# Where the first local query of the next image is convolved, normed and stacked: within the dense stage instead of the last slots of the image ahead

## The chip, the cores and the metric

One core of a Trainium2 chip runs the whole kernel. The metric is the device time of that core in microseconds, as the median of several runs. One further execution was recorded by the hardware profiler; times of single instructions come from that one. Engines are called PE (TensorE, matmuls), PEld (its weight loads), DVE (VectorE), ACT (ScalarE), POOL (GpSimd) and SP (SyncE, which here only issues DMAs).

## What is computed

The input is four images of 384 channels and 48 x 48 pixels. Every image goes through one attention block whose queries get a local part from a depthwise 7 x 7 convolution (all in fp32):

```python
local = conv_general_dilated(x, conv_w, feature_group_count=C)   # depthwise 7x7, then a batch norm as scale and shift
x_norm = layernorm(x_flat, ln_gamma, ln_beta)                    # over the 384 channels of a pixel
q, k, v = split(x_norm @ qkv_w.T + qkv_b)                        # 8 heads of 48
q = q + layernorm(local_flat, ln_gamma, ln_beta)
attn = softmax(q @ k.T * 48 ** -0.5)
out = x_flat + (attn @ v) @ proj_w.T + proj_b
```

## The kernel before

**Tiles and stages.** The 48 rows of an image are cut into 6 groups of 8 rows, 384 pixels each. A query tile t is one group of one image, so there are 24, and tile t belongs to image t // 6. An array over channels is `[128, 3, 384]`: 128 partitions, 3 chunks of channels, 384 pixels. The work of an image has two kinds of stage.

- The *dense stage* (loop `for gk in range(NG)` at the start of an image's first tile, line 1042) makes keys, values and queries of the image group by group from the normed x, and the output projections of the image before. `from_x` yields twelve times for a group; each call of `both(making)` lets it run over one pair of projections, so a group has six pairs. For the first image this work is written out ahead of the loop over tiles.
- Then each of its six tiles runs 12 *slots*. A slot takes one pair of heads and 6 blocks of 128 keys: `score_batch` (matmuls at L884, then the exponentials on ACT at L892) and `weigh_batch` (matmuls at L899 with the exponentials and the values). Three slots make a pair of heads.

PE, DVE and ACT run their instructions in the order in which the program writes them. The DMAs on SP and POOL are put in an order by the framework's scheduler, which knows their inputs; within each queue they are then issued in that order, and a DMA whose input isn't ready holds the ones behind it.

**The convolution.** `conv_ops(t)` is a generator of 147 DVE instructions for tile t (49 taps of 3 chunks, L288 and L284). All tiles' generators are chained into one `stream`, which runs ahead of the tile that is being attended. `convolve(point)` takes the next so many of them. How many, `plan` works out before: each point in the program (two a slot, five a group of the dense stage) has a `room`, an estimate in us of the DVE time left there (`spare`, `spare_at_keys`), and each tile has a point at which its convolution is `due`. At each point the plan takes the highest rate that any coming due point asks for. A new tile's first instruction also issues the load of the slab of x for the tile after it (`load_slab`, SP, two buffers); the results go to `acc`, of which there are three buffers.

**The norm of the convolved tile** (class `Norm`) is done without matmuls, in steps that are written at different places:

- `sum` adds the three chunks on DVE (L404, L405); `out` transposes and reduces (L460, L461), sends 12 numbers a partition to DRAM (`parts`, L464) and reads them back in the form that sums over partitions (`four`, L465). This exchange is the way of one norm's sums across the partitions; each norm has two.
- `few_centre` waits for `four` (L474) and subtracts the mean (L481, L482); `squares` runs on ACT; `sum_squares` and `out` make the second exchange.
- `few_variance` waits for it (L474, L488); `few_root` is three small ACT instructions (L493 to L495); `few_newton` refines on DVE (L499 to L501).
- `local_end` scales the tile (L734). `query_end` adds it, times the gain, to the query projected from x (L743, three instructions).

The tiles of x for the next image are normed in the same way, under the names `norm_x` (in slots) and `norms_x` (in the dense stage).

**Stacking.** fp32 scores are made of rounded high and low parts. `high_queries(t, p)` rounds on ACT (L756), `low_queries(t, p)` subtracts on DVE (L761) and then issues six SP DMAs (four for the last pair of heads) that put the parts into the rows in which the matmuls want them (L766, L768). `gather_tails` (L517) collects the fourth pair of heads with eight SP DMAs. Every score matmul of a slot reads the stacked query `qs` of its pair of heads. `qs` has five buffers, which residual loads (`load_residual`) and fetched outputs (`fetch`) share.

**Order today.** For tile t + 1 the norm is in the slots of tile t: `sum` at the end of slot 4, `few_centre` at the end of slot 5, `sum_squares` at the end of slot 6, `few_variance` in slot 8, `local_end` in slot 9. Its convolution is due before slot 5. `query_end`, `high_queries` and `low_queries` follow in slot 9 only if t + 1 belongs to the same image. For the first tile of the next image the projected query does not exist yet, so `query_end` stands in group 1 of the dense stage, `high_queries` at its end, and `low_queries` and `gather_tails` at the end of group 2:

```python
            if following and s == second + 1:
                local_end(t + 1, norm.few_newton() if t else norm.newton())
                if g < NG - 1:
                    query_end(t + 1)
                    high_queries(t + 1, 0)
```

In the dense stage `lows_out` makes the low parts of a group's keys (L599) and issues their DMAs: for key chunk 0 eight on SP (`ks<-k`, L533 to L536), for the others on POOL. `finish` adds an output's residual (L865) and stores it from SP (L868).

Of the kernel before, what the change touches and what calls it, by code (L numbers as in the profile page):

```python
# [45 lines left out]
def unshifted_pass(  # L46
# [265 lines left out]
    def norm_slots(t):  # L312
        return (5, 8) if t else (8, 10)

    def spare(t, s, half):
        b, g = divmod(t, NG)
        first, second = norm_slots(t)
        time = 3.6 - (0.0 if half else 0.6) - (0.6 if half and s % 3 == 1 else 0.0)
        if b + 1 < B and g >= later(b + 1):
            time -= {(3, 1): 2.3, (4, 1): 2.2, (5, 1): 2.3, (7, 0): 0.4, (8, 0): 2.6}.get(  # L320
                (s, half), 0.0
            )
        if g:
            time -= {(2, 0): 0.7, (4, 1): 1.4}.get((s, half), 0.0)
        if t == 0:
            time -= {(7, 1): 1.1, (8, 1): 1.4, (9, 1): 1.1, (11, 0): 5.0}.get((s, half), 0.0)
        elif t + 1 < NT:
            time -= {(4, 1): 2.3, (5, 1): 2.2, (6, 1): 2.3, (8, 0): 0.4, (9, 0): 4.5}.get(
                (s, half), 0.0
            )  # L330
        return max(0.3, time)
# [5 lines left out]
    def spare_at_keys(b, g, h):  # L337
        time = 4.6 - {0: 0.6, 2: 0.7, 3: 1.4, 4: 1.2}.get(h, 0.0)
        if g < later(b):
            time -= {0: 2.3, 2: 2.2, 4: 2.3}.get(h, 0.0)  # L340
        if 0 < g <= later(b):
            time -= {1: 0.4, 3: 2.6}.get(h, 0.0)
        return time - {(1, 1): 2.7, (2, 1): 1.4}.get((g, h), 0.0)

    points, room = [], []
    for t in range(NT):
# [3 lines left out]
        points += [("slot", t, s, h) for s in range(NSLOT) for h in range(2)]  # L350
        room += [spare(t, s, h) for s in range(NSLOT) for h in range(2)]
    each = CC * KS * KS
    due = [
        (points.index(("slot", t - 1, norm_slots(t - 1)[0], 0)), t * each) for t in range(1, NT)
    ]
    share = {}

    def plan(done):
# [10 lines left out]
    def convolve(*point):  # L369
        for _ in range(share[point]):  # L370
            next(stream)
# [265 lines left out]
    def both(making):  # L637
        next(making)
        next(making)
# [92 lines left out]
    def local_end(t, rs):  # L732
        acc = accs[t]
        nc.vector.scalar_tensor_tensor(acc, acc, -1.0, rs, ALU.mult, ALU.mult)  # L734
# [300 lines left out]
    for t in range(NT):  # L1035
        b, g = divmod(t, NG)
        if g == 0 and b:

            sums_add()
            load_x(b, NG - 1)  # L1040
            norms_x = {}
            for gk in range(NG):
                before = t - NG + gk
                load_residual(before)
                making = from_x(b, gk, before, ao if gk < NG - 1 else outputs[before][0])
                new = NG - later(b) + gk if gk < later(b) else None
                old = norms_x.get(gk - 1)
                both(making)
                convolve("kv", t, gk, 0)
                if new is not None:  # L1050
                    norms_x[gk] = Norm(xn[b, new])
                    norms_x[gk].sum()
                    norms_x[gk].out()
                both(making)
                if old:
                    old.few_variance()
                    old.few_root()
                if gk == 1:
                    query_end(t)
                    rb = divide(t - 1)  # L1060
                if gk == 2:
                    last_ao = outputs[t - 1][0]
                    nc.vector.tensor_mul(last_ao, last_ao, rb)
                convolve("kv", t, gk, 1)
                both(making)
                convolve("kv", t, gk, 2)
                lows_out(1)
                if new is not None:
                    norms_x[gk].few_centre()
                    norms_x[gk].squares()  # L1070
                both(making)
                convolve("kv", t, gk, 3)
                lows_out(2)
                if old:
                    old.scale(old.few_newton())
                both(making)
                convolve("kv", t, gk, 4)
                if new is not None:
                    norms_x[gk].sum_squares()
                    norms_x[gk].out()  # L1080
                both(making)
                if gk == 1:
                    high_queries(t, 0)
                if gk == 2:
                    low_queries(t, 0)
                    gather_tails(*reversed(queries[t]))
                if gk < NG - 2:
                    ao = fetch(before + 1)
        following = t + 1 < NT
        next_image = b + 1 < B  # L1090
        coming = next_image and g >= later(b + 1)
        first, second = norm_slots(t)
        for s in range(NSLOT):
            pair, third = divmod(s, KB // BATCH)
            if third == 1 and pair < NP - 1:
                high_queries(t, pair + 1)
            score_batch(t, s)
            if pair < NP - 1 or g < NG - 1:
                load_keys(b, (pair + 1) % NP, third)
            if s == 1 and g == 0:  # L1100
                keep_stack(b)
            if s == 2 and g:
                rb = divide(t - 1)
            if s == 0 and coming:
                load_x(b + 1, g - later(b + 1))
            if s == NSLOT - 4 and g == NG - 1:
                if next_image:
                    ao = fetch(t - g)
                    for gx in range(NG - later(b + 1), NG - 1):
                        load_x(b + 1, gx)  # L1110
                else:
                    places = [("acc", 3)] * 3 + [("sq", 2)] * 2 + [("qs", 5)]
                    aos = []
                    for i in range(NG):
                        load_residual(t - g + i, *places[i])
                        aos.append(fetch(t - g + i) if i < g else outputs[t][0])
            if coming and s == X_SLOTS[1] + 1:
                norm_x.scale(norm_x.few_newton())
            if following and s == second + 1:
                local_end(t + 1, norm.few_newton() if t else norm.newton())  # L1120
                if g < NG - 1:
                    query_end(t + 1)
                    high_queries(t + 1, 0)
            if coming and s == X_SLOTS[0] + 1:
                jobs.extend(norm_x.square_jobs())
            if following and s == first + 1:
                jobs.extend(norm.square_jobs())
            if coming and s == X_SLOTS[1]:
                norm_x.few_variance()
            if t and following and s == second:  # L1130
                norm.few_variance()
            convolve("slot", t, s, 0)
            sums_add()
            if t == 0 and s in (first, second):
                norm.mean_kept()
            if coming and s == X_SLOTS[1]:
                norm_x.few_root()
            if following and s == second:
                norm.few_root() if t else norm.root()
            if s == first and t == 0:  # L1140
                norm.centre()
            weigh_batch(t, s)
            if third == 1 and pair < NP - 1:
                low_queries(t, pair + 1)
            convolve("slot", t, s, 1)
            if following and s == second + 1 and g < NG - 1:
                low_queries(t + 1, 0)
                gather_tails(*reversed(queries[t + 1]))
            if coming and s == X_SLOTS[0]:
                norm_x.few_centre()  # L1150
            if t and following and s == first:
                norm.few_centre()
            if s == OUT_SLOT and g:
                ao = outputs[t - 1][0]
                nc.vector.tensor_mul(ao, ao, rb)  # L1155
                hold(t - 1)
            if coming and s == X_SLOTS[0] - 1:
                norm_x = Norm(xn[b + 1, g - later(b + 1)])
                norm_x.sum()
                norm_x.out()  # L1160
            if coming and s == X_SLOTS[0] + 1:
                norm_x.sum_squares()
                norm_x.out()
            if following and s == first - 1:
                norm = Norm(accs[t + 1])
                norm.sum()
                if t:
                    norm.out()
            if following and s == first + 1:
                norm.sum_squares()  # L1170
                if t:
                    norm.out()
# [559 lines left out]
```

## Time and profile before

| | us |
|---|---|
| median of 3 runs | 2858.98 |
| lowest and highest | 2855.88, 2863.1 |
| the profiled execution, its own time | 2855.57 |
| its span in the profile | 2853.8 |
| PE busy | 2769.0 (97%) |
| DVE busy | 2459.7 (86%) |
| ACT busy | 1636.8 (57%) |
| granted PE clock, mean over the span | 0.985 |

A busy figure is the time in which an engine has an instruction running; matmuls overlap, so a busy PE need not be at its peak. Tile t's slots begin, by the first score matmul of each tile, at 164.8 us for tile 0, 280.8 for tile 1, 690.9 for tile 5, 931.9 for tile 6, 1607.9 for tile 12 and 2283.2 for tile 18. The dense stages of images 1, 2 and 3 end at the last three of these times.

### The profile page before, as it was taken

The numbers are of one execution on the slowest core, as the hardware profiler recorded it, in microseconds if no ns is written. First come the engines' busy times: TensorE is split into PE (matmuls) and PEld (weight loads), VectorE is DVE, ScalarE is ACT, GpSimd is POOL, SyncE is SP. The second block draws the span as 40 slices with busy tenths as digits, with TensorE's granted clock in tenths as the row PEclk, the third lists the DMA queues.
The fourth block names the chain that finished last, engine by engine and source line by source line (L and its number), as shares of the span: only waits on it lengthen the run. The fifth ranks groups of instructions, "written<-read, shape, count | busy, mean of one in ns | idle before, by whom it ended". The sixth has DMA issues, their size and how long they took to land.

```text
span 2853.8 us, 53591 instructions
## 1 busy us (share of the span) xinstructions
PE 2769.0 (97%) x19238; PEld 1740.4 (61%) x19238; DVE 2459.7 (86%) x4875; ACT 1636.8 (57%) x2638; POOL 592.9 (21%) x1125
## 2 busy tenths in 40 slices
PE   9987989999899999999999999999999999999999
PEld 6654656565555666665655666666665566666665
DVE  7789998989899999997998999998888998998502
ACT  4344656565522666676642467666672276676662
POOL 5720000000057200010026401000005710010000
PEclk9998999999999999999999999999999999999999
DMA  7444444553445554445536545455454555444541
GB/s 140 106 135 117 125 128 134 151 151 101 140 117 162 166 175 140 149 144 162 153 100 182 166 144 155 168 157 145 133 150 133 153 159 167 149 144 167 163 161 63
DMA packets 197461, 410.57 MB, mean 144 GB/s; under 512 B 69888, under 2 KB 140480, under 8 KB 196672
## 3 DMA queue, kind: packets, MB, share of 16 engines
q0 software_dynamic: 65440, 254.88, 26.7%
q1 hardware_dynamic: 128752, 148.55, 21.2%
q8 instruction: 154, 2.52, 0.4%
q10 hardware_dynamic: 2992, 3.62, 0.4%
q14 instruction: 123, 1.01, 0.1%
HBM read 298.44 MB, written 64.78 MB: 127 GB/s over the span
## 4 chain that ended last, share of the span: by engine, by line
PE 78%; DVE 14%; DMA 5%; issue 1%; ACT 0%; SPq 0%; POOL 0%; ACTq 0%; DVEq 0%; POOLq 0%
PE o L899 32%; PE r L884 26%; PE r L511 20%; DVE acc L288 10%; DMA parts<-part 2%; DMA four<-parts 2%; DMA qs<-qs 1%; DVE sq L405 0%; DVE sq L460 0%; DVE ao L803 0%; DVE part L461 0%; DMA start_up<-in_qkv_wT_dram 0%; DVE sq L404 0%; DVE acc L482 0%; DVE ao L1155 0%
## 5 line engine op out<-in xcount | busy, mean ns | idle before, releaser
L288 DVE SCALAR_TENSOR_TENSOR acc<-slab,vec,acc 128x368 f32<-128x368 f32 (+6 forms) x3447 | 1767.1, 581 | 1.2
L892 ACT ACTIVATE pt<-r 128x768 f32<-128x768 f32 x1728 | 1250.0, 829 | 150.2 <-PE r L884 120.7
L899 PE MATMUL o<-pt,v 128*64 128x384 f32 x6912 | 1184.4, 492 | 0.0
L884 PE MATMUL r<-qs,ks 64*128 64x384 f32 x10368 | 1016.7, 345 | 67.0 <-DMA qs<-qs 38.9
L884 PEld LDWEIGHTS r<-qs,ks 64*128 64x128 f32 x10368 | 905.9, 188 | 256.9 <-issue 210.6
L899 PEld LDWEIGHTS o<-pt,v 128*64 128x64 f32 x6912 | 473.0, 137 | 592.9 <-issue 516.0
L568 POOL DMA_DIRECT2D ks<-wide x276 | 199.3, 724 | 1819.4 <-PE r L884 1768.6
L784 ACT COPY o<-o 113x384 f32<-113x384 f32 x192 | 91.9, 479 | 379.0 <-PE o L899 379.0
L511 PE MATMUL r<-xn,w_qk 128*128 128x384 f32 x864 | 283.7, 486 | 0.0
L511 PEld LDWEIGHTS r<-xn,w_qk 128*128 128x128 f32 x864 | 164.3, 190 | 114.3
L511 PE MATMUL r<-w_v,xn 128*128 128x384 f32 x432 | 145.1, 488 | 0.7 <-ACT w_v L697 0.5
L588 ACT COPY v<-r 128x384 f32<-128x384 f32 x72 | 32.1, 480 | 193.0 <-PE r L511 193.0
L803 DVE TENSOR_TENSOR ao<-ao,o 113x384 f32<-113x384 f32 x144 | 79.4, 551 | 54.8 <-ACT o L784 54.7
L511 PE MATMUL r<-af,w_o 128*128 128x384 f32 x360 | 119.1, 487 | 0.0
L511 PEld LDWEIGHTS r<-w_v,xn 128*128 128x128 f32 x432 | 81.6, 190 | 59.2 <-issue 2.4
L474 DVE TENSOR_REDUCE few<-four 128x12 f32<-128x48 f32 x80 | 18.5, 231 | 107.9 <-DMA four<-parts 107.5
L794 ACT COPY ao<-o 113x384 f32<-113x384 f32 x72 | 34.5, 479 | 125.4 <-PE o L899 125.4
L536 POOL DMA_DIRECT2D wide<-k x192 | 96.7, 508 | 9.2 <-issue 5.5
L511 PEld LDWEIGHTS r<-af,w_o 128*128 128x128 f32 x360 | 68.3, 190 | 47.8 <-issue 0.6
L558 POOL DMA_DIRECT2D wide<-k x192 | 93.1, 491 | 9.5 <-DMA wide<-k 6.8
L552 POOL DMA_DIRECT2D wide<-k x144 | 70.6, 493 | 97.6 <-ACT k L596 69.2
L613 ACT ACTIVATE xn<-r,qkb 128x384 f32<-128x384 f32 x72 | 40.8, 578 | 78.1 <-PE r L511 76.6
(129 smaller groups left out, 1160.7 us busy)
## 6 DMA issues: line engine op xcount, KB each, us to landing
ks<-wide POOLq DMA_DIRECT2D x276, 768.0 KB, 7.1
qs<-qs SPq DMA_DIRECT2D x528, 48.0 KB
xr<-in_x_dram SPq DMA_DIRECT2D x24, 576.0 KB
slab<-in_x_dram SPq DMA_DIRECT2D x32, 378.0 KB
wide<-k POOLq DMA_DIRECT2D x480, 24.0 KB, 2.1
held<-ao SPq DMA_DIRECT2D x20, 576.0 KB
af<-held SPq DMA_DIRECT2D x20, 576.0 KB
rb<-rden SPq DMA_DIRECT2D x48, 216.0 KB
```

Of the source, the lines that this page charges most:

```text
L288: nc.vector.scalar_tensor_tensor(dst, src, weight, dst, ALU.mult, ALU.add)
L511: nc.tensor.matmul(dst, lhsT=weights(c), rhs=src(c), start=c == 0, stop=c == CC - 1)
L536: queue.dma_start(out=dst[r + 32 * i : r + 32 * i + 32, 1], in_=k[r + 16 : r + HD, 1])
L552: nc.gpsimd.dma_start(out=last[16 * u : 16 * u + 16, 0], in_=k[r : r + 16, 0])
L558: nc.gpsimd.dma_start(out=last[to : to + 16, 1], in_=k[r : r + 16, 1])
L568: nc.gpsimd.dma_start(out=stacks[b, p].bitcast(F32)[:, :, at], in_=wide[b, p][:, :, at])
L613: nc.scalar.activation(src[:, i, :], q[:, :G], AF.Identity, bias=qkb[:, 0, i : i + 1])
L784: nc.scalar.copy(part[0 : 64 + HA], sums[0 : 64 + HA, 0, :G])
L803: nc.vector.tensor_add(dst, dst, part[0 : 64 + HA])
L884: nc.tensor.matmul(r[:, j, :G], lhsT=ks[rows, w, kb * P : (kb + 1) * P], rhs=qs[rows, m, :], start=i == 0, stop=i == 2,)
L892: nc.scalar.activation(pt, r[:, :, :G], AF.Exp, scale=SCALE)
L899: nc.tensor.matmul(sums[halves[j], 0, :G], lhsT=values[t // NG, kb // NB][:, first : first + 64], rhs=pt[:, j, :], start=i == 0, stop=i == ...
```

## The change

For the first tile of images 1, 2 and 3 (tiles 6, 12 and 18) the whole norm moves from the slots of the tile ahead (5, 11 and 17) into groups 4 and 5 of the dense stage, and `query_end` and the stacking move there too, from groups 1 and 2 to group 5. The point at which the convolution of these tiles is due moves to the start of group 4, and the estimates of room follow; the shares of all points change with that. In the last tile of an image nothing is done for a following tile any more. Every other tile's order stays.

```diff
@@ in spare, spare_at_keys and the due points
-        elif t + 1 < NT:
+        elif g < NG - 1:
...
-        return time - {(1, 1): 2.7, (2, 1): 1.4}.get((g, h), 0.0)
+        return time - {
+            (1, 1): 1.0, (2, 1): 1.4, (4, 0): 2.3, (4, 2): 2.2, (4, 4): 2.3, (5, 0): 0.4,
+            (5, 1): 4.5, (5, 2): 0.6,
+        }.get((g, h), 0.0)
...
-    due = [
-        (points.index(("slot", t - 1, norm_slots(t - 1)[0], 0)), t * each) for t in range(1, NT)
-    ]
+    due = []
+    for t in range(1, NT):
+        last = ("slot", t - 1, norm_slots(t - 1)[0], 0) if t % NG else ("kv", t, 4, 0)
+        due.append((points.index(last), t * each))
@@ in the dense stage, for gk in range(NG)
                     norms_x[gk].sum()
                     norms_x[gk].out()
+                if gk == 4:
+                    norm = Norm(accs[t])
+                    norm.sum()
+                    norm.out()
                 both(making)
...
                 if gk == 1:
-                    query_end(t)
                     rb = divide(t - 1)
+                if gk == 5:
+                    norm.few_variance()
+                    norm.few_root()
...
                 convolve("kv", t, gk, 1)
+                if gk == 5:
+                    local_end(t, norm.few_newton())
+                    query_end(t)
+                    high_queries(t, 0)
                 both(making)
                 convolve("kv", t, gk, 2)
                 lows_out(1)
...
+                if gk == 4:
+                    norm.few_centre()
+                    norm.squares()
+                if gk == 5:
+                    low_queries(t, 0)
+                    gather_tails(*reversed(queries[t]))
                 both(making)
...
+                if gk == 4:
+                    norm.sum_squares()
+                    norm.out()
                 both(making)
-                if gk == 1:
-                    high_queries(t, 0)
-                if gk == 2:
-                    low_queries(t, 0)
-                    gather_tails(*reversed(queries[t]))
...
-        following = t + 1 < NT
+        following = g < NG - 1
@@ in the slots
                 local_end(t + 1, norm.few_newton() if t else norm.newton())
-                if g < NG - 1:
-                    query_end(t + 1)
-                    high_queries(t + 1, 0)
+                query_end(t + 1)
+                high_queries(t + 1, 0)
...
-            if following and s == second + 1 and g < NG - 1:
+            if following and s == second + 1:
                 low_queries(t + 1, 0)
```

## The prediction

> **What bounds the kernel now.** I read the busy time by stage first, one window for each query tile, because the page's 97% for PE is a mean over stages with different limits. Columns: window, its length, then busy us (instructions) of PE, PEld, DVE, ACT, POOL, then granted PE clock, DMA share, GB/s.
>
> ```profile
> 280.80:382.40 101.60, 95.05 (x720) 61.10 (x720) 94.52 (x186) 61.12 (x93) 8.65 (x12) 0.94 0.42 120
> 382.40:487.70 105.30, 95.49 (x724) 60.36 (x722) 97.70 (x192) 61.38 (x94) 8.64 (x12) 0.94 0.43 130
> ...
> 586.50:690.90 104.40, 94.47 (x724) 59.09 (x722) 91.57 (x192) 62.67 (x100) 8.64 (x12) 0.95 0.46 133
> 690.90:792.40 101.50, 93.88 (x723) 59.38 (x721) 89.29 (x184) 62.63 (x99) 5.13 (x16) 0.95 0.43 127
> 792.40:931.90 139.50, 139.50 (x434) 82.08 (x432) 131.33 (x255) 34.75 (x72) 89.50 (x184) 1.00 0.54 147
> 931.90:1020.50 88.60, 88.60 (x721) 56.65 (x720) 85.73 (x168) 60.36 (x93) 15.98 (x27) 1.00 0.54 167
> ```
>
> Rows one to four are tiles 1, 2, 4 and 5 (image 0), then the first dense stage, then tile 6. An undisturbed tile takes 88.3 us of unbroken matmuls; the dense stage is also unbroken. Image 0's tiles take 99 to 105 us. The list of waits, asked for VectorE in the same windows, says who sets that: in tile 5 DVE waited 11.1 us for `four<-parts`, in tile 4 11.8, in tile 2 7.0, in tile 1 6.5. Busy plus that wait is 100.4 of 101.5 us in tile 5, 103.4 of 104.4 in tile 4, 104.7 of 105.3 in tile 2: **VectorE sets image 0, TensorE everything after it.**
>
> The wait in tile 5 belongs to the very norm that the change moves. Timeline of VectorE, then of TensorE:
>
> ```profile
> 737.59 0.55 DVE L803 TENSOR_TENSOR ao<-ao,o 113x384 f32<-113x384 f32 x1
> 749.23 0.23 DVE L474 TENSOR_REDUCE few<-four 128x12 f32<-128x48 f32 x1 [11.09 <-DMA four<-parts]
> ...
> 747.22 1.84 PE L884 MATMUL r<-qs,ks 64*128 64x384 f32 x18
> 753.27 0.79 PE L884 MATMUL r<-qs,ks 64*128 64x384 f32 x6 [4.21 <-ACT ao L794]
> 754.39 2.29 PE L884 MATMUL r<-qs,ks 64*128 64x384 f32 x12 [0.33 <-ACT pt L892]
> 756.61 6.14 PE L899 MATMUL o<-pt,v 128*64 128x384 f32 x24
> ```
>
> VectorE waits at `few_centre`, ScalarE's squares of that norm wait behind it, and PE stalls; the 24 `weigh` matmuls after it take 6.14 us, not 4.09.
>
> Last, the nearest thing to what the change builds: the start, where the query of tile 0 is stacked right at the end of the first dense work. TensorE, VectorE, then SP's queue:
>
> ```profile
> 164.83 0.65 PE L884 MATMUL r<-qs,ks 64*128 64x384 f32 x1 [8.31 <-issue]
> 166.34 5.20 PE L884 MATMUL r<-qs,ks 64*128 64x384 f32 x35 [0.85 <-DMA qs<-qs]
> ...
> 152.76 1.14 DVE L743 SCALAR_TENSOR_TENSOR xn<-acc,of_ln,xn 128x384 f32<-128x384 f32 x2
> 157.57 0.56 DVE L761 TENSOR_TENSOR qs<-xn,qs 128x384 fp32r<-128x384 f32 x1 [3.67 <-ACT qs L756]
> ...
> 152.87 3.04 SPq L517 DMA_DIRECT2D qt<-xn  x5
> 157.56 0.51 SPq L768 DMA_DIRECT2D qs<-qs  x1
> 162.99 1.49 SPq L768 DMA_DIRECT2D qs<-qs  x2
> ```
>
> `query_end` ends at 153.9, `low_queries` at 158.1, the last stacking DMA is issued by 164.5, and scores run freely from 166.34: **12.4 us after `query_end`, 8.2 after `low_queries`.** Today the other images pay none of this, since their first query is stacked in groups 1 and 2, over 60 us ahead.
>
> **What the Trainium skill says.** "TensorE: Matmul & The Clock Gate", section "What's actually happening": after an idle window of about 3.4 us the clock falls to half and needs a busy window to return. The trace agrees: the granted clock is 0.83 over 748 to 768 us, around that stall, so 3.4 us lost on top of its 4.5 us of idle time. "DMA: Bandwidth & Descriptors", section "Issuing engines are not separate DMA queues": DMAs of SP and POOL share the same 16 engines. The trace agrees: `four<-parts`, 24 KB, landed 11 us after its issue while a slab and key stacks were moving. "Perfetto Trace Analysis", section "Sequencer Loop": an engine takes instructions in order and each waits for its semaphores; so a late one holds all behind it, as in tile 5.
>
> **The change, part by part.** The plan's shares are worked out from the code's own arithmetic; a conv instruction costs 0.52 us by pace (25 in 12.87 us).
>
> *Conv moved out of image 0.* Tiles 1 to 4 get 1, 4, 3 and 12 instructions fewer: 20 x 0.52 = 10.4 us, all on VectorE where it sets the time: **-10.4**.
>
> *Tile 5.* Removed: `sum` and `sum_squares` with `out` (2 x 2.3), `few_centre` (2.1), `few_variance` (0.4), newton and `local_end` (2.3): 9.4 us, and the wait of 11.1. Added: 4 conv, 2.1. VectorE falls from 100.4 to about 82, under TensorE's 88.3. The tile ends at 88.3 to 90: **-12**. The norm of x stays there; a wait of up to 4 us of its own would fit in the room.
>
> *Tiles 11 and 17* lose the same norm for 12 and 15 conv. They stand at 89.8 and 88.8: at most **-2**. Tiles 18 to 21 get 6 to 8 conv more (4 us); VectorE is at 80 to 82 of 88.3 there, tile 6 ran unbroken at 85.7, so 0; without that room up to 4 us each.
>
> *Tiles 10 and 16.* The next conv tile, so its slab load, now begins at slot 5, between the two exchanges of their norm; before it began at slot 1. VectorE waited 8.0 us for one exchange in tile 10, which cost that tile 5.0 us. Tile 4, with the slab there, took 11.2 us from part to four, tile 10 without it 11.4, tile 5 with it 13.8. So 0 to 2.5 us more each, times 1.3 for the clock: **+3** (0 to +7). A gain is excluded, as no instruction left that stretch.
>
> *Dense stages, VectorE's sum.* 19, 19 and 12 conv fewer (10 us) against 9.4 us of norm: 0. `query_end`, the copies and stacking DMAs only change place within the stage. Group 4 now has two exchanges; those of x in this stage took 5.3 to 7.9 us from part to landing, and some 7 us of other VectorE work lies between, so waits of 0 to 2. In the first dense stage tile 8's slab load comes right behind the second exchange, as in tile 5: 8 to 11 us there.
>
> *Dense stages, the end.* Let E be the end of dense matmuls (931.9, 1607.9, 2283.2). ScalarE evacuates the second pair of group 5 by E-14.4. `few_root` queues behind it: 0.75, E-13.65. Newton, `local_end`, `query_end`: 4.2 us in the rows from 997.84 to 1001.93, so E-9.4. ScalarE's `high_queries` follows at E-8.9; it waits for `query_end`, and the evacuation of keys 1 and 2 waits behind it, some 3 us later than now, covered by free PSUM buffers. Then 6 conv (3.1), one `low` (0.6), `low_queries` (0.55): E-5.2. SP has 20 issues of 0.62 us in this stretch: 8 of `gather_tails` and 2 stackings that need only the high part, from E-10.4 to E-4.3; 6 `ks<-k` of the same `low`, to E-0.6; the 4 stackings left, to E+1.9. They land 1.9 us (the start) to 5 us (tile 5's stacking) later: **E+5.4** by the middle. Nothing hides it: all scores of slot 0 need this query. Groups' output additions, later on VectorE by as much, hold the fourth PSUM buffer until about E+4, so an early landing would not make it free.
>
> *Buffers and POOL.* The query's `qs` buffer is free for four groups longer, and `acc` of tile 6 is held four groups longer: three are in use when tile 8 begins in group 5, tile 9 begins in slot 11, after tile 7's is freed. POOL's stores of keys 1 and 2 start some 3 us later; those keys are wanted from slot 3 on. PE waited for none of these in the dense stage, so 0 either way.
>
> The second stage adds 0 to 2.4 for its second exchange (middle 1.2), the first 2 to 5 (3.5): waits of 5.4, 6.6 and 9, sum 21. By tile 5's stall (4.5 idle, 3.4 lost at half clock) and the one at 271.85 (8.9 idle, 10.2 us at half rate, so 5.1), the clock adds 3.4, 3.4 and 5.1: **+33** (from 12 to 50).
>
> *Sum:* -10.4 - 12 - 2 + 3 + 33 = **+12 us**, 0.4%. The profiled execution took 2855.57 us (span 2853.8), so 2867.6 by it; the median of the runs shown, 2858.98, stands 3.4 above it: 2871.
>
> **Rivals.** *The query is in time* (not slower): if SP issues the stackings before `ks<-k` and they land in 2 us, slot 0 begins by E+1.5 with no half clock. Then three times 1.5 plus 3 minus 24.4 is -17: 2842. It decides against my forecast once the three starts together cost under 21 us. For it: two high stackings can be issued early, and PE loses nothing below a stall of 2 us. Against it: in tile 6, SP issued all eight gathers (1000.89 to 1008.5) ahead of the stackings. *SP blocked longer*: if SP's order puts the stackings behind the group's three output stores, which wait for VectorE until about E+5, they land at E+11, with 5.1 of clock each: 48 + 3 - 24.4 = +27, 2886. For it: that queue holds stores waiting at 907 to 911 us now. Against: the stores come later in program order. *Image 0 keeps its time*: if tile 4's stalls are of latency (11.8 us of exchange) more than of work, and tile 5's other exchange waits instead, half the gain is lost: +24, 2883. Against: busy and waits fill the tile with 1 us to spare.
>
> **How the numbers follow.** About 0.3%, 8.6 us, is what a measurement of this kernel can tell from no change. Forecast 45% (own range 2859 to 2885, mostly above 8.6 us), query in time 20%, SP blocked 20%, image 0 unchanged 15%. Faster: nearly all of the first rival, 0.20. Same: the forecast's low third and some of the last rival, 0.25. Slower: the rest, 0.55. Range 2842 to 2892: from the first rival's value to a little past the blocked one.
>
> **What would show it.** Tile 5 near 89 us with no wait on `four<-parts` over 5; tile 4 near 98; the first score of tiles 6, 12 and 18 waiting 5 to 9 us for `qs<-qs`, with a clock of 0.8 to 0.9 in slot 0. A start of slot 0 without a wait, or tiles 1 to 5 at their old lengths, would make the prediction wrong.

## The result and the profile after

| | before | after |
|---|---|---|
| median of 20 runs, us | 2858.17 | 2865.03 |
| lowest and highest | 2846.92, 2869.02 | 2856.48, 2871.35 |
| the profiled execution, its own time | 2855.57 | 2862.87 |
| its span | 2853.8 | 2861.1 |
| granted PE clock, mean | 0.985 | 0.984 |

The ratio is 1.0024, 95% interval 1.0013 to 1.0035: the changed kernel is slower by about 6.9 us. That is less than the 0.3% which the prediction took for the least that can be told, but the interval leaves out no change. The two profiled executions differ by 7.3 us, so their tiles can be set against each other. Lines of the changed code stand 4 higher: L884 is now L888, L474 is L478, L766 and L768 are L770 and L772, L464 and L465 are L468 and L469.

First the busy times by stage of the kernel after (window, length, busy us and instructions of PE, PEld, DVE, ACT, POOL, then PE clock, DMA share, GB/s). The rows are tiles 1, 2, 4 and 5, the first dense stage, tile 6 and, new here, tile 9.

```profile
280.50:382.30 101.80, 94.76 (x722) 60.81 (x722) 94.05 (x185) 61.12 (x93) 8.65 (x12) 0.94 0.41 120
382.30:487.10 104.80, 94.67 (x724) 60.20 (x722) 94.41 (x186) 61.40 (x94) 8.65 (x12) 0.93 0.44 131
...
591.00:692.10 101.10, 93.39 (x724) 59.28 (x722) 88.33 (x185) 62.74 (x100) 8.64 (x12) 0.95 0.48 139
692.10:780.50 88.40, 88.40 (x723) 56.80 (x722) 81.71 (x170) 60.38 (x94) 5.13 (x16) 1.00 0.53 151
780.50:920.40 139.90, 139.41 (x432) 81.88 (x432) 126.71 (x245) 35.98 (x76) 88.00 (x180) 1.00 0.50 137
920.40:1010.90 90.50, 89.07 (x722) 56.82 (x722) 87.69 (x173) 60.35 (x93) 17.91 (x31) 1.00 0.52 162
...
1190.70:1288.90 98.20, 92.23 (x722) 59.31 (x720) 87.20 (x176) 63.15 (x100) 8.65 (x12) 0.95 0.47 139
```

Tile 5 has become an unbroken tile: 88.4 us with PE busy throughout. Tile 1 is no shorter than before although VectorE has a little less to do, and tile 2 only 0.5 us shorter with 3.3 us less of VectorE; tile 4 is 3.3 us shorter with 3.2 us less. Tile 6 has lost 1.8 us at its head. Tile 9 takes 98.2 us at a clock of 0.95; before it took 88.3. By tiles, from first score to first score (tiles 5, 11 and 17 with the dense stage behind them):

| tiles | before | after | difference |
|---|---|---|---|
| 1 to 4 | 410.1 | 411.6 | +1.5 |
| 5, with the dense stage | 241.1 | 228.4 | -12.7 |
| 6, 12, 18 | 88.6, 88.5, 88.5 | 90.4, 91.4, 91.5 | +7.8 |
| 11, 17, each with the dense stage | 229.3, 228.3 | 228.4, 228.6 | -0.7 |
| 10, 16 | 93.3, 93.7 | 90.1, 89.3 | -7.6 |
| 8, 9, 15, 20 | all 88.3 | 91.6, 98.2, 93.9, 89.1 | +19.6 |
| all others | | | -0.6 |
| sum | | | +7.3 |

Each dense stage ends with 0.6 us of idle PE, so the starts cost 9.6 us rather than 7.8; that part stands in the rows of tiles 5, 11 and 17. The loss that makes the kernel slower is that of tiles 8, 9, 15 and 20, in which the change wrote nothing new.

**The head of tile 6.** Dense matmuls end at E = 919.9, and the first score starts at 920.45. The timeline of TensorE after, then that of VectorE, then SP's queue:

```profile
920.45 0.41 PE L888 MATMUL r<-qs,ks 64*128 64x384 f32 x1 [0.53 <-DMA qs<-qs]
921.58 0.63 PE L888 MATMUL r<-qs,ks 64*128 64x384 f32 x4 [0.72 <-DMA qs<-qs]
922.87 3.11 PE L888 MATMUL r<-qs,ks 64*128 64x384 f32 x31 [0.66 <-DMA qs<-qs]
```

```profile
902.48 0.23 DVE L478 TENSOR_REDUCE few<-four 128x12 f32<-128x48 f32 x1 [0.88 <-DMA four<-parts]
...
906.05 0.17 DVE L503 TENSOR_TENSOR few_u<-few_u,few 128x12 f32<-128x12 f32 x1 [3.13 <-ACT few_u L499]
...
914.22 0.55 DVE L765 TENSOR_TENSOR qs<-xn,qs 128x384 fp32r<-128x384 f32 x1
```

```profile
909.66 0.52 SPq L772 DMA_DIRECT2D qs<-qs  x1
914.33 0.52 SPq L538 DMA_DIRECT2D ks<-k  x1
...
918.12 0.53 SPq L770 DMA_DIRECT2D qs<-qs  x1
918.70 0.59 SPq L772 DMA_DIRECT2D qs<-qs  x1
919.33 0.59 SPq L770 DMA_DIRECT2D qs<-qs  x1
919.97 1.23 SPq L772 DMA_DIRECT2D qs<-qs  x2
921.24 5.02 SPq L521 DMA_DIRECT2D qt<-xn  x8
```

The norm's second exchange held VectorE for 0.88 us only. `low_queries` (L765) ends at 914.77, E-5.1, and SP issues the six `ks<-k` ahead of the last stackings, whose issue ends at 921.2, E+1.3. Scores run freely from 922.87, E+3.0, 1.7 us after that last issue: three small stalls, together 1.9 us, and no half clock. In tile 12 two stalls of 0.53 and 1.02 us, and in tile 18 three of 0.69, 0.59 and 0.38, were each followed by 3.4 us at half clock.

**Tile 9.** SP's queue in the kernel before, and then in the kernel after. `rden` and `rb` are the way of the softmax's reciprocals: 12 KB go to DRAM and are read back spread out over the partitions.

```profile
1210.50 0.34 SPq L827 DMA_DIRECT2D rden<-rd  x1
1211.98 0.34 SPq L832 DMA_DIRECT2D rb<-rden  x1
...
1224.08 0.60 SPq L464 DMA_DIRECT2D parts<-part  x1
1226.11 0.57 SPq L465 DMA_DIRECT2D four<-parts  x1
1227.51 0.55 SPq L768 DMA_DIRECT2D qs<-qs  x1
```

```profile
1209.47 2.20 SPq L94 DMA_DIRECT2D slab<-in_x_dram  x4
1211.77 0.38 SPq L831 DMA_DIRECT2D rden<-rd  x1
1224.89 0.31 SPq L836 DMA_DIRECT2D rb<-rden  x1
...
1227.35 0.60 SPq L468 DMA_DIRECT2D parts<-part  x1
1230.45 0.58 SPq L469 DMA_DIRECT2D four<-parts  x1
1231.15 0.55 SPq L772 DMA_DIRECT2D qs<-qs  x1
...
1234.18 1.22 SPq L772 DMA_DIRECT2D qs<-qs  x2
```

Tile 9 starts at 1197.05 before and at 1190.70 after. Before, `rb` follows `rden` by 1.5 us. After, `rden` is issued right behind the four DMAs of a slab, and `rb`, which needs it landed, goes out 13.1 us later; in all that time SP issues nothing. Counted from the tile's start, `parts`, `four` and the stackings leave 9.6 to 10.7 us later than before. TensorE after, at the next pair of heads:

```profile
1237.74 0.41 PE L888 MATMUL r<-qs,ks 64*128 64x384 f32 x1 [2.85 <-DMA qs<-qs]
1240.27 1.01 PE L888 MATMUL r<-qs,ks 64*128 64x384 f32 x4 [2.12 <-DMA qs<-qs]
1242.28 5.45 PE L888 MATMUL r<-qs,ks 64*128 64x384 f32 x31 [1.01 <-DMA qs<-qs]
```

There are 6.0 us of stalls here on stackings, and 31 matmuls in 5.45 us against 3.11 in the head of tile 6: PE ran at half clock, in a stretch of 10.2 us from 1238.2. The row of tile 9 above adds up: 98.2 us less 92.2 busy is the 6.0 idle, and 92.2 is 4.0 over an unbroken tile's 88.3; together the tile's 9.9.

The slab stands there because the plan's shares moved. A tile's first convolution instruction asks for the next tile's slab. By the end of the first dense stage 35 instructions fewer have been issued than before, so the next beginnings fall later: that of tile 10's convolution moves from slot 9 of tile 7 to slot 0 of tile 8, that of tile 11's from slot 11 of tile 8 to slot 1 of tile 9.

### The profile page after: what moved, and what is told of

Same layout as the page of the kernel before. It is cut to its first block, busy times and chain, and to the rows that moved or that the text cites. A ratio compares the mean times of both kernels' runs of the same rounds, so it can differ in the third digit from the quotient of the medians.

```text
span 2861.1 us, 53602 instructions
## 1 busy us (share of the span) xinstructions
PE 2771.2 (97%) x19238; PEld 1742.0 (61%) x19238; DVE 2458.6 (86%) x4875; ACT 1635.9 (57%) x2632; POOL 592.4 (21%) x1125
## 3 DMA queue, kind: packets, MB, share of 16 engines
q14 instruction: 123, 1.01, 0.1%
## 4 chain that ended last, share of the span: by engine, by line
PE 69%; DVE 18%; DMA 8%; POOL 2%; issue 1%; ACT 1%; SPq 1%; DVEq 0%; ACTq 0%; POOLq 0%
PE o L903 30%; PE r L888 26%; PE r L515 13%; DVE acc L288 13%; DMA parts<-part 2%; DMA four<-parts 2%; DMA wide<-k 1%; DMA qs<-qs 1%; DMA slab<-in_x_dram 1%; POOL wide L540 0%; DVE ao L807 0%; DVE sq L409 0%; DVE qs L765 0%; DMA start_up<-in_qkv_wT_dram 0%; DVE k L603 0%
## 5 line engine op out<-in xcount | busy, mean ns | idle before, releaser
L888 PE MATMUL r<-qs,ks 64*128 64x384 f32 x10368 | 1020.8, 345 | 73.2 <-DMA qs<-qs 38.9
L888 PEld LDWEIGHTS r<-qs,ks 64*128 64x128 f32 x10368 | 908.8, 188 | 264.5 <-issue 203.2
L478 DVE TENSOR_REDUCE few<-four 128x12 f32<-128x48 f32 x80 | 18.5, 231 | 124.9 <-DMA four<-parts 124.7
```

The costliest lines, as they stand in the source:

```text
L888: nc.tensor.matmul(r[:, j, :G], lhsT=ks[rows, w, kb * P : (kb + 1) * P], rhs=qs[rows, m, :], start=i == 0, stop=i == 2,)
```

## The experiments

Two theories stood against each other. *Loads*: the change as such is a small gain, and the loss comes from slab loads that the changed shares put ahead of SP's short round trips. *Norm*: the loss comes from the norm and the stackings in their new place.

**The loads' place, in both kernels.** In the program, loads that come due in slots 0 to 9 are held until slot 10, in the changed kernel and in the kernel before. This edit is called the hold:

```diff
     def conv_ops(t):
...
-            load_slab(*divmod(t + 1, NG))
+            asked.append(t + 1)
+            if not holding[0]:
+                slabs_in()
@@ in each slot
+            holding[0] = s < 10
+            if not holding[0]:
+                slabs_in()
```

> The changed kernel, except that a slab load that falls due in slots 0 to 9 of a tile is issued at slot 10. Theory A (the loss in tiles 8, 9 and 15 comes from where the shifted conv boundaries put the slab load, ahead of SP's short round trips): tiles 9 and 15 fall from 98.2 and 93.9 us to 89 or less, tile 8 from 91.6 to 89, and the whole by 10 to 18 us, to about 2850. Image 0's tiles 1 to 4, where the slab lies between a norm's two DMAs, lose part of their waits for four<-parts as well (some 5 us in all). Theory B (those tiles are late because VectorE has one or two conv instructions more in each): nothing changes by more than 3 us.

> The kernel before, with the same delay of slab loads to slot 10. Theory A: tiles 10 and 16 fall from 93.3 and 93.7 us to 89 or less, since their slab load stands at slot 1 as that of tiles 9 and 15 does after the change; the whole falls by 9 to 15 us, to about 2847, so that the move by itself is then worth under 5 us either way. Theory B: no change beyond 3 us.

The changed kernel with the hold took 2847.14 us, ratio to the kernel before 0.9962 (0.9947 to 0.9976); the kernel before with the hold 2848.43, 0.9969 (0.9955 to 0.9982). So the edit is worth 17.7 us to the changed kernel (1.0024 less 0.9962, times 2858) and 8.9 to the one before. But it did not do what both expectations assume: in neither trace does a load move to slot 10. In the changed kernel the slab still goes out 8.8 us into tile 8 and 14.9 us into tile 9, where it went out after 8.3 and 18.8 us without the hold; in the kernel before it still goes out 14 us into tile 10. The framework's scheduler left the beginnings of these loads within 4 us of where they had been. What the edit changed is their place among their neighbours on SP. The queue in tile 8 of the changed kernel (the tile starts at 1099.13), then with the hold (1094.16):

```profile
1107.43 1.95 SPq L94 DMA_DIRECT2D slab<-in_x_dram  x4
...
1113.79 0.35 SPq L826 DMA_DIRECT2D rd<-den  x1
1115.86 0.35 SPq L831 DMA_DIRECT2D rden<-rd  x1
```

```profile
1102.37 0.53 SPq L834 DMA_DIRECT2D rd<-den  x1
1102.95 0.89 SPq L94 DMA_DIRECT2D slab<-in_x_dram  x2
...
1108.11 0.51 SPq L839 DMA_DIRECT2D rden<-rd  x1
1108.67 0.43 SPq L94 DMA_DIRECT2D slab<-in_x_dram  x1
```

`rd<-den` brings the sums that VectorE inverts for `rden`. VectorE's waits in this tile, in the changed kernel and with the hold (waited us, times, longest):

```profile
DVE few L478 <- DMA four<-parts: 7.6, 1, 7.6
DVE rd L827 <- DMA rd<-den: 2.7, 1, 2.7
```

```profile
DVE few L486 <- DMA four<-parts: 1.7, 1, 1.7
```

VectorE, ScalarE and GpSimd run the same instructions in the same order in both; the order of SP's queue alone differs. With the whole load ahead of `rd`, tile 8 takes 91.6 to 96.5 us in the four profiles of the changed kernel that have this order (both unchanged ones and two of the versions below). With `rd` ahead of it, tile 8 takes 88.3 in all three that have that order. So for tile 8 the load's place on the queue is shown to be the cause, and not the norm.

In tile 9 the hold puts `rden` ahead of the load too, and `rb` follows after 1.7 us; the tile falls from between 96.0 and 98.2 us to between 94.0 and 94.8, in the same profiles. The other 6 us of its loss stay, with VectorE still waiting 8 to 9 us for one `four<-parts`; they are not explained. Tile 15 takes 88.7 us in this profile. In the kernel before, the hold brings tile 16 from 93.7 to 88.3 us but leaves tile 10 at 94.1, which missed the expectation. Between the two edited kernels the change comes to -2 us, uncertain by 6; with the loads still there, this is not the worth of the change without them.

**Which loads.** The same hold, in the program, for the loads due in slots 0 to 2 only, and for those due in slots 3 to 9 only:

```diff
-            holding[0] = s < 10
+            holding[0] = s < 3 or (asked and s < 10)    # slots 0 to 2
...
+            holding[0] = 3 <= s < 10                    # slots 3 to 9
```

> The changed kernel; only slab loads that fall due in slots 0 to 2 (conv boundaries in tiles 8, 9, 14, 15, 20 and 21) are delayed to slot 10. If the 17.7 us that delaying all of them gained come from these, where the load stands ahead of divide's round trip through SP, this version gains 12 us or more on the changed kernel (about 2850). If they come from loads between a norm's two DMAs in slots 3 to 9, it gains under 5.

> The complement: only slab loads that fall due in slots 3 to 9 (tiles 1 to 5, 10, 11, 16 and 17) are delayed to slot 10. If the loads ahead of divide are the cause, this gains under 5 us on the changed kernel; if those within the norm's exchanges are, 12 us or more (about 2850), with waits for four<-parts in tiles 1 to 4 shorter than the 7 to 12 us of the changed kernel.

The early ones: 2849.38 us, 0.9966 (0.9955 to 0.9976), nearly all of the gain. The others: 2862.53, 1.0009 (0.9997 to 1.002), at most a small part; tile 9 takes 97.9 us there, tile 8 95.5. Again no load moved to slot 10, and the two versions don't part the loads as their expectations say: both have the load of tiles 2 and 3 split on the queue (two DMAs, then one, then one), though the first edit doesn't name these loads. In tiles 8, 9, 15 and 20 only the first has it split. SP's queue in tile 9 with the early ones held (the tile starts at 1180.63):

```profile
1194.92 0.54 SPq L839 DMA_DIRECT2D rden<-rd  x1
1195.51 0.42 SPq L94 DMA_DIRECT2D slab<-in_x_dram  x1
1196.62 0.33 SPq L844 DMA_DIRECT2D rb<-rden  x1
```

The round trip takes 1.7 us again, with one piece of the slab behind `rden` instead of the whole ahead of it. Tile 9 loses 6.3 us all the same: VectorE waits 10.8 us for `four<-parts`, in two waits. So the blocked `rb` isn't all of that tile's trouble, and a good part of this version's gain lies in tiles 1 to 4: 402.7 us, against 411.6 in the changed kernel. The version with the others held has 402.2 there, so the difference between the two lies behind image 0; tiles 8 and 9 make 10.6 us of it.

**The shares alone, in the kernel before.** Norm, query and stacking stay where they were. The numbers of convolution instructions in tiles 6 to 9 are those of the changed kernel. The first dense stage gets 105, not the 121 that the expectation names: tiles 1 to 5 keep their old numbers, which are 16 more in sum, so that the convolutions of tiles 9 to 11 begin at the same points as in the changed kernel. The edit:

```diff
+            if point in fixed:                  # the dense stage and tiles 6 to 9
+                done = float(given + fixed[point])
```

> The kernel before with its norm, query and stacking where they were; only the numbers of convolution instructions in the first dense stage and in tiles 6 to 9 are those of the changed kernel (121 instead of 140 in the stage; the convolution of tile 8 begins in group 5, of tile 9 at slot 11 of tile 6, of tile 10 at slot 0 of tile 8, of tile 11 at slot 1 of tile 9). So the slab loads stand in tiles 8 and 9 where the changed kernel has them, and nothing else of the change is there. Theory A (the changed shares put the slab loads ahead of the short SP round trips of divide and stacking): tile 8 takes 1 to 7 us more than 88.3, tile 9 takes 93 to 98 us instead of 88.3, rb<-rden follows rden<-rd by over 8 us in tile 9, and the kernel takes about 2867 us, ratio 1.002 to 1.005. Rival B (tiles 8 and 9 lose time through the moved norm or the later stacking of tile 6's query, and the shares are harmless): both tiles at 88.3 and ratio 1.000 within 0.001. Tile 10 may change either way by up to 4 us.

Tile 8 took 94.5 us and tile 9 97.5. SP's queue in this tile 9, from 1200.51:

```profile
1218.64 1.95 SPq L94 DMA_DIRECT2D slab<-in_x_dram  x4
1220.69 0.41 SPq L842 DMA_DIRECT2D rden<-rd  x1
1232.29 0.31 SPq L847 DMA_DIRECT2D rb<-rden  x1
```

The same order and nearly the same wait, 11.6 us, with nothing of the norm moved. So the shifted shares alone rebuild the loss of both tiles, and *Norm* falls there. TensorE's stalls in tile 9 are not all the same ones: here 3.7 us for ScalarE and 1.1 for stackings, in the changed kernel 6.0 for stackings. The whole took 2884.14 us, 1.0101 (1.0082 to 1.012), more than expected: tiles 10 and 11 lost another 7.0 and 6.8 us. The 30 instructions left undone by then are made up for there, 20 in tile 10 and 10 in tile 11, which I had priced at 4 us at most. That they are the cause is likely but not shown, since the loads of these two tiles moved too.

**A failed attempt at the same.** I first tried to bring the load into tiles 9 and 15 of the kernel before by calling it there:

```diff
+    late = {12: (9, 1), 18: (15, 1)}
-        if t + 1 < NT:
+        if t + 1 < NT and t + 1 not in late:
...
+            for t_slab, at in late.items():
+                if at == (t, s):
+                    load_slab(*divmod(t_slab, NG))
```

> The kernel before, in which only the slab loads for conv tiles 12 and 18 are issued later, at slot 1 of tiles 9 and 15, where the changed kernel issues its own. All conv shares and the norm stay. Theory A: tile 9 grows from 88.3 to about 98 us and tile 15 from 88.3 to about 94, the whole by about 15 us. Theory B: both stay at 88.3.

It took 2858.02 us, 1.0002 (0.9992 to 1.0013), with both tiles at 88.3. But its trace has no slab load on SP from 5 to 45 us of tile 9: the framework's scheduler had issued it where it stood before, at the end of tile 8. The situation wasn't built, and the run says nothing for or against either theory.

**The order of issue at the starts.** In group 5 `low_queries` is written ahead of the keys' low parts:

```diff
+                if gk == 5:
+                    low_queries(t, 0)
                 lows_out(1)
...
                 if gk == 5:
-                    low_queries(t, 0)
                     gather_tails(*reversed(queries[t]))
```

> The changed kernel with one edit: in group 5 of the dense stage low_queries is written ahead of lows_out(1), so that the query's stackings can stand ahead of the six ks<-k DMAs in SP's queue. Theory A (the starts of tiles 6, 12 and 18 wait for the last stackings, which SP issues only after ks<-k): the three starts lose 1 to 2 us each instead of 1.8 to 3.1, the dense stages with tiles 11 and 17 end 0.6 us earlier, and the kernel takes 2 to 6 us less than the changed one, ratio to the kernel before about 1.001. Rival B (the starts wait for the landing alone, whatever the order of issue): no difference, ratio 1.0024. Tiles 8, 9 and 15 should keep their loss in both theories.

SP's queue, then TensorE, at the head of tile 6 (E = 918.6):

```profile
912.97 0.51 SPq L770 DMA_DIRECT2D qs<-qs  x1
...
914.79 0.59 SPq L772 DMA_DIRECT2D qs<-qs  x1
915.47 0.54 SPq L538 DMA_DIRECT2D ks<-k  x1
```

```profile
918.54 3.22 PE L888 MATMUL r<-qs,ks 64*128 64x384 f32 x30
922.80 0.79 PE L888 MATMUL r<-qs,ks 64*128 64x384 f32 x6 [1.05 <-DVE xr L869]
```

The stackings are all issued by E-3.2 and no score waits for them; what is late next is the output addition on VectorE, which frees the fourth PSUM buffer at E+4.2. Tiles 6, 12 and 18 take 90.0, 89.5 and 89.3 us, and the dense stages no longer end in idle time. The time, 2860.72 us, 1.0017 (1.0006 to 1.0029), is 2 us under the changed kernel's ratio, which the intervals can't tell from nothing; the traces side with the order of issue.

**Both edits together**, the hold and the order:

> The changed kernel with slab loads delayed to slot 10, and with low_queries ahead of the group's first low key in group 5, so that SP gets the stackings before six of the key loads. The prediction's step says that these six issues (3.7 us) stand ahead of the stackings; then the first score of tiles 6, 12 and 18 starts without a wait, slot 0 has no half clock, and the three starts lose under 2 us each instead of about 3: 3 to 6 us less than with the delayed slab loads alone (2847.1), so about 2842. If the output additions on VectorE hold the starts, or the stackings are not earlier for it, it stays within 2 us of 2847.

2844.11 us, 0.9939 (0.9919 to 0.9958): faster than the kernel before by 17 us and than the changed one by 24, and the fastest version run. Tiles 6, 12 and 18 take 90.1, 89.7 and 89.4 us, without half clock at their heads, as expected. The interval overlaps that of the hold alone, so the step from there (0.9962) is not clear of noise.

**Image 0.** The changed kernel with the old numbers of convolution in tiles 0 to 4, timed, and later profiled once more:

```diff
+            rooms, dues = (room0, due0) if point[1] < NG and point[0] == "slot" else (room, due)
-            ahead = [(sum(room[i:end]), n - done) for end, n in due if end > i]
+            ahead = [(sum(rooms[i:end]), n - done) for end, n in dues if end > i]
```

> The changed kernel, but the conv instructions of tiles 0 to 4 as many at each point as in the kernel before (20 more than in the changed kernel); the rest of the plan follows from there. By the prediction's sum, VectorE sets these tiles and they take 10 us more than in the changed kernel (tiles 1 to 4 together 421.6, not 411.6). By the rival (the exchange through DRAM has a length of its own, and conv that leaves the stretch in front of it turns into waiting for it), tiles 1 to 4 stay within 3 us of 411.6, and tile 5 stays at 88 to 89 since its norm is gone.

> The changed kernel with the old numbers of convolution instructions in tiles 0 to 4, profiled a second time, because the first profile (2849.2 us) was of the fastest of its ten executions, whose median is 2863.25, and showed tiles 8, 9 and 15 at 88.3. Theory A (in most executions the loads of slabs hold up tile 8 or 9 there too): tiles 8 and 9 together take 5 us or more over 176.5, and the whole 2860 to 2870 us. Rival B (the usual executions lose the time in image 0, whose convolution was put back): tiles 1 to 4 take 416 us or more, and 8 and 9 stay at 88.3.

2863.25 us, 1.0022 (1.0009 to 1.0035), the changed kernel's ratio. The first profile has tiles 1 to 4 at 411.7 us, the second, of an execution of 2863.83, at 415.8, with tiles 8 and 9 at 88.3 and 88.7, tile 15 at 93.1 and tile 20 at 91.7. Theory A was wrong about which tiles, and rival B missed its 416 by a hair. The run does not isolate image 0: tile 5 takes about 5 us more here, and the convolutions in tiles 8 and 9 begin elsewhere. In tile 9 the load stands ahead of six stackings and only then comes `rden`; the tile takes 88.3 and 88.7 us. So here a load early in the tile did not by itself cost time.

**How far executions differ.** Both kernels were profiled a second time, unchanged.

> The kernel before, profiled a second time, to see how far its tiles differ from one execution to the next. Theory A: tiles 8, 9, 15 and 20 stay at 88.3 within 0.5 us, tiles 10 and 16 within 1 us of 93.3 and 93.7, and tiles 1 to 4 within 6 us of 410. Rival B (tiles 8, 9 or 15 lose time in some executions of the kernel before as well): one of them is over 90 us, and then their loss in the changed kernel is no effect of the change.

> The changed kernel once more, for one look: which of its tiles repeat. What the program's order fixes should repeat within 1 us (tile 5 at 88.8, the starts of tiles 6, 12 and 18 with 2 to 3 us of wait); if the 98.2 us of tile 9 and the 93.9 of tile 15 come from how transfers happen to fall, they should differ by several us, as tile 3 did between the kernel before (98.8) and its version with two slab loads moved (104.0), whose programs are the same up to there.

The kernel before: 2855.45 us, tiles 8, 9, 15 and 20 at 88.3, tiles 1 to 4 at 411.5. The changed one: 2868.1 us, tiles 8, 9, 15 and 20 at 94.6, 97.3, 93.6 and 91.8, 24.2 us more than four unbroken tiles. So their loss belongs to the change and not to one execution, though tiles 15 and 20 are also seen at 88.3 to 88.7 in versions with the changed kernel's queue order there. What does differ is tile 3: 98.8 us and 102.8 in two executions of the kernel before.

## Why the prediction was right, and where it was wrong

The forecast was slower, at 2871 us; it came to 2865.03. The sign was right and the sum near, but that is luck, by errors that offset each other: the starts, which carried the forecast, were priced some 23 us too high, image 0 some 8 to 12 us too favourably, an effect of +20 was missing, and one of -8 had been put at +3. By the prediction's own signs it is half right: tile 5 ran free, but the first scores of tiles 6, 12 and 18 waited 0.4 to 1.0 us at a time, not 5 to 9, and tile 4 took 101.0 us, not 98.

- **Tile 5: right.** -12 predicted; -12.7 measured, and the tile takes 88.4 us. It ran free although the exchange of x that stays there still had VectorE wait 3.3 us.
- **Starts: mechanism right, size wrong.** +33 predicted, 9.6 measured. The order (six `ks<-k`, then the last stackings) and the times (`low_queries` ending at E-5.2, measured E-5.1; last issue at E+1.9, measured E+1.3 in tile 6) held; but in tile 6 five stackings came last, not four, and all eight gathers came behind them, where I had them ahead. The mis-sized terms are the landing, 1.7 us after the last issue where I took the middle of 1.9 and 5; the waits for the exchanges in the first stage, 0.88 us where I took 3.5; and so the clock, 0, 3.4 and 3.4 us at half rate, of which half is lost, 1.7 each, where I took 3.4, 3.4 and 5.1 lost. In the second profile it was 3.4, 0 and 3.4. That an early landing would meet the fourth PSUM buffer, held until about E+4, was right (E+4.2).
- **Conv moved out of image 0: wrong.** -10.4 predicted; +1.5 between the two profiles. Over more executions: six with the old numbers in these tiles (the two of the kernel before, the shares alone, the failed attempt, image 0 put back twice) take 410.1, 411.5, 408.7, 413.5, 411.7 and 415.8 us, mean 411.9; three with the new ones (the changed kernel twice, the order of issue) 411.6, 408.7 and 409.9, mean 410.0. So about 2 us. By tiles this is uneven: between the same profiles tile 4 gained 3.6 us on average, tile 3 lost 2.6, and tiles 1 and 2 changed by less than 1. I had read "busy plus wait fills the tile" as work that sets the time, but the wait is no constant. VectorE's waits in tiles 2 and 4 of the kernel after (waited us, times, longest):

```profile
DVE few L478 <- DMA four<-parts: 9.8, 1, 9.8
...
DVE few L478 <- DMA four<-parts: 11.7, 2, 10.6
```

  In tile 2 VectorE's work fell by 3.3 us and the wait rose from 7.0 to 9.8; in tile 4 the wait stayed (11.8 before). So in tile 2 the work taken away became waiting, as the rival *image 0 keeps its time* has it; in tile 4 the work fell by 3.2 us, the wait stayed, and the tile got shorter, as I had priced it. What sets tile 3 is open. The order of SP's queue matters here as well: the four versions of the changed kernel with a hold run the same instructions in tiles 1 to 4, with the load split in tiles 2 and 3 as the only difference, and take 402.2 to 405.7 us there, against 408.7 to 411.6. With the hold in the kernel before it is 409.3, from one profile and with the queue in another order in tiles 3 and 4; how much of the 10.4 us the new numbers are worth with a split load is not shown.
- **Tiles 10 and 16: wrong sign.** +3 predicted, -7.6 measured. I excluded a gain because no instruction left that stretch. The slab load's move was priced only for what it comes near, not for what it leaves: it left the place right ahead of `rden`, the place that it takes in tile 9 after the change. In tile 10 the longest wait for an exchange fell from 8.0 to 3.3 us. For tile 16 the kernel before with the hold points to that place: with `rden` ahead of the last two of the load's DMAs it took 88.3 us in one profile, against 92.6 to 93.7 in four with the whole load ahead. Tile 10 took 94.1 us with the hold, so its cause stays open.
- **Tiles 8, 9, 15 and 20: not in the sum.** The plan's later beginnings were worked out for tiles 10 and 16 and the buffers, and for the other tiles I priced only 4 us of instructions, at nothing. The load that each beginning asks for, 792 or 1008 KB a slab, was not followed past SP's short round trips. For tiles 8 and 9 it is shown that the shares make the loss, since they alone rebuild it. That the load's place on the queue does it is shown for tile 8, and for about a third of tile 9's loss. Tile 20 points the same way: it takes 88.3 to 91.8 us in six profiles with the load ahead of `rd`, over 89 in five of them, and 88.3 to 88.4 in three with `rd` ahead. For tile 15 the cause is open: with the load right ahead of `rden` it takes 88.3, 88.7 and four times 93.1 to 93.8 us, with `rden` ahead 88.7, 94.0 and 94.4.
- **Dense stages, buffers, POOL: right.** VectorE's sum cost nothing there; the stage grew by the 0.6 us at its end alone.

## What to carry to other kernels

When a change shifts a schedule, follow the bulk transfers that the shifted steps issue, not only the shifted instructions: ask which short store-and-read-back comes right behind each on the same queue. Work taken from an engine that ends up waiting for a transfer can turn into waiting, so look at what ends last in each tile. After moving a DMA in the program, look in the trace where the queue issued it: twice here the scheduler left it where it was, and once the time improved all the same, for another reason than the one intended. And write the query that the next stage starts with ahead of transfers that are wanted later.

## What the runs showed of the hardware

- In tile 9 of the kernel before, 1.5 us passed from the issue of a 12 KB store on SP to that of the read-back which needs it. Right behind a slab's four DMAs, 792 KB, it took 10.0 to 13.1 us in tile 9 of the five profiles with this order, but only 4.9 to 5.6 us in tile 15 of six profiles: the order allows the delay and does not fix its size. In tile 9 the queue stood still meanwhile, since the read-back was next in its order.
- Stalls of 2.85, 2.12 and 1.01 us, a few matmuls apart, were followed by 10.2 us of half clock. Short ones go either way: at the head of tile 6, 0.53, 0.72 and 0.66 us brought none in one execution of the changed kernel, and 0.54, 0.71 and 0.63 brought 3.4 us in the other. Single stalls of 1.76 and 1.88 us in the kernel before were followed by 3.4 us of half clock, one of 2.19 us in the kernel after by none. None of these stalls reached the 3.4 us of the idle window in the prediction.
- The same program's tile 3 took 98.8 and 102.8 us in two executions, while undisturbed tiles agree within 0.05 us: a tile in which engines wait for exchanges isn't to be read from one profile.
